# Odd heads' values in the rows of even heads' sums, one output product per tile, and gates that read a column with stride zero

## Chip, core and metric

The kernel runs on one core of one Trainium2 chip. The metric is the device time of one execution in microseconds (us); less is better. The profile records one execution: TensorE (PE, its weight loads PEld), VectorE (DVE), ScalarE (ACT), GpSimd (POOL) and SyncE (SP, which issues DMAs). All data are 32-bit floats, apart from a mask in bf16.

## What is computed

The input x has 16 batches of 256 tokens with 128 features. Six blocks are applied to it, each on a layer norm of x and each added to x:

```python
x = x + 0.5 * ffn0(layernorm(x))        # 128 -> 512 -> 512 -> 512 -> 128: silu * linear, gelu, gelu
x = x + attn0(layernorm(x))             # theta(x) phi(x)^T g(x) / sqrt(128), no softmax
x = x + 0.5 * ffn0(layernorm(x))
x = x + 0.5 * moe(layernorm(x))         # gates from the first token: top 2 of 8 experts, rank 64
x = x + attn1(layernorm(x))             # 16 heads of 8, rotary, causal softmax, W_O
x = x + 0.5 * moe(layernorm(x))
```

In attn1 each of the 16 heads has scores = q k^T / sqrt(8) under a causal mask, a softmax over the keys, and out = attn v; the heads are concatenated to 128 features and multiplied by W_O. In moe the gates are logits = first_token @ Wr^T, the two largest of 8, and a softmax over these two; the two chosen experts are merged into one 128 x 128 matrix per batch.

## The kernel before, in words

The 16 batches are worked in nine groups: seven of two batches (four tiles of 128 tokens) and two of one. Each group passes the feed-forward twice ("which" 0 and 1 in the code). The order of feed-forwards on PE is fixed: groups 0 and 1 for the first time, then alternately a second pass of group g and the first pass of group g + 2. The linear attention of a group (`nonlocal_attn`, L547) follows its first pass. After its second pass come `experts` (L644), `attention` (L703) and `after_attention` (L931).

No instruction order is written out by hand. Every piece of work is a generator that yields steps (L230) with an engine, an estimated time, buffers to take, and needs. The loop at the end of the kernel takes, again and again, the step that can begin first by its own clocks, and records its instructions; a step made with `either` (L238) takes the engine that would finish it first. Five constants steer this: LOAN (a penalty for banks 0 to 3 of PSUM), SPARED (a penalty on DVE in `either`), PATIENCE (how long exp's function table waits), SLACK (how close two steps are to count as equal), and LATE (how many of the last groups use a finer order: even heads first, and each half of the output normalised by itself). So a changed step or constant moves instructions on all engines. All recorded instructions have one line, L222, in the profile. While feed-forwards remain, PE's queue holds their products between those of the attention; when none is left, the loop adds products of `ident` by `ident` that only keep PE's clock up (`awake`, L1026).

The attention of one batch: `rotary` (L684) makes queries and keys; `maxima` (L760) makes the scores once and takes each row's maximum for each head; the negative maxima are transposed and added as a feature to the queries (`queries_with`, L805); `weighted` (L825) makes the scores again, transposed, in four rounds j of four heads each, takes exp on ACT (`softmax`, L836, reading PSUM into the tile pr) and clears the upper triangle on POOL. `values` (L868) then multiplies pr by the tile vm. For each tile of keys, vm holds 16 blocks of 32 columns, four row groups r by four rounds j. In the block of round j the eight columns at 16 * (j // 2) hold the head's values, the eight columns behind them hold ones, and the other sixteen zeros. Rounds 0 and 2 add up into one half of a PSUM bank, rounds 1 and 3 into the other half (w columns each, w = 256 queries for a whole batch). So in every 32 rows of a half there are 8 rows of outputs, 8 rows of the sums of exp that belong to them, and again 8 and 8. `output` (L849) transposes the 32 x 32 blocks (den), takes the reciprocal of two sums per block (rec), spreads it over 16 columns, transposes back (inv) and multiplies (oT). The rows with sums become 1 and meet rows of zeros in wo, which is W_O^T spread over 2 x 128 rows by `_by_half` (L1154). So the output needs two products per tile of 128 tokens, one for each half (L912 to L917).

`gated` (L582) makes the gates of a group: a product of cls (the first token's features, repeated in 128 columns) by wrT with 8 columns for each batch, then the two largest on DVE, a gather of the two experts' rows by POOL, and their product, added to ident (we). In `experts` cls is copied out of xnT, repeated, by POOL or DVE. In `gated_ahead` (L659) the first token's row y after attention is computed early and turned into a column by a product with a row of 128 ones, which gives the column repeated; ACT or DVE copies it from PSUM.

Of the kernel before, what the change touches and what calls it, by code (L numbers as in the profile page):

```python
# [20 lines left out]
P = 128  # L21
# [6 lines left out]
LANDING = 2.2  # L28
LOAN = 0.5
SPARED = 0.2  # L30
PATIENCE = 4.0
SLACK = 0.02
HOP = {"PE": 0.24, "ACT": 0.15, "DVE": 0.12, "POOL": 0.08}
# [8 lines left out]
NG = len(BATCHES)  # L42
LATE = 3
SPLIT = 0
# [12 lines left out]
def macaron_kernel(ctx: ExitStack, tc: tile.TileContext, a: dict, out: bass.AP):  # L57
# [54 lines left out]
    wvT = load("wvT", [P, D], a["wvT"], nc.sync)  # L112
    wo = load("wo", [P, 2, D], a["wo"].rearrange("(h p) d -> p h d", p=P), nc.sync)
    cosT = load("cosT", [P, S], a["cosT"], nc.sync)
# [7 lines left out]
    causal = cst.tile([P, P], F32, name="causal")  # L122
    ones = cst.tile([1, P], F32, name="ones")
    pht = cst.tile([P, D], F32, name="pht")
# [47 lines left out]
    def slots(n, name, shape):  # L172
# [14 lines left out]
        "mx": slots(2, "mx", [P, 2, P]),  # L187
    }
    extra = [cst.tile([P, 3, 2, 2 * P], F32, name=f"hS{l}") for l in (1, 2)]
    for n in ("vm", "mx", "rot"):  # L190
# [3 lines left out]
    def constants():  # L194

        yield step("POOL", 1.4, needs=(("in", 0, 0),))
        nc.gpsimd.memset(causal, 0.0)
        nc.gpsimd.affine_select(
            out=causal, in_=causal, compare_op=ALU.is_ge, fill=NEG, base=0, pattern=[[-1, P]], channel_multiplier=1
        )  # L200
        nc.gpsimd.memset(ones, 1.0)
        yield step(None, 0.0, sets=(("constants",),))

        for b in store_of["vm"]:
            yield step("POOL", 1.8)
            nc.gpsimd.memset(b.t, 0.0)
            yield step("POOL", 0.6, drop=(b,))
            for j in range(4):
                o = 8 + 16 * (j // 2)
                nc.gpsimd.memset(b.t.rearrange("p t r j c -> p (t r) j c")[:, :, j, o : o + DK], 1.0)  # L210
        for b in store_of["mx"]:
            yield step("POOL", 0.3, drop=(b,))
            nc.gpsimd.memset(b.t, 0.0)
# [368 lines left out]
    def gated(nb, cls):  # L582
# [3 lines left out]
        for b in range(nb):  # L586
            nc.tensor.matmul(pl[:, b, :], cls[:, b, :], wrT, start=True, stop=True)
        yield step("DVE", 0.5 + 0.4 * nb, drop=(bk,))
# [55 lines left out]
    def experts(sg):  # L644
        xn = yield from normed(sg.t0, sg.n, (("ffn", 0, (1, sg.t0)), ("ffn", 1, (1, sg.t0)), ("constants",)))
        xnT = yield from by_feature(sg.n, xn)
        if sg.first:
            nb = len(sg.parts)
            yield either(("POOL", 0.2 + 0.1 * nb), ("DVE", 0.1 + 0.1 * nb))
            cls = sml.tile([P, 2, P], F32, name="cls", bufs=2)  # L650
            by().tensor_copy(
                cls[:, :nb],
                xnT.t[:, : sg.n * P].rearrange("p (b s) -> p b s", b=nb)[:, :, 0:1].to_broadcast([P, nb, P]),
            )
            merged["before", sg.g] = yield from gated(nb, cls)
            yield step(None, 0.0, sets=(("before", sg.g),))
        yield from applied(("before", sg.g), sg, xnT)

    def gated_ahead(g, nb, y):  # L659
# [9 lines left out]
        for b in range(nb):  # L669
            nc.scalar.activation(  # L670
                y[:, b, :], y[:, b, :], AF.Identity, bias=shift[:1, b : b + 1], scale=rstd[:1, b : b + 1]
            )
        (bk,) = yield pe(0.22 * nb, banks=1)
        pc = bk.t[:, : 2 * D].rearrange("p (b d) -> p b d", b=2)
        for b in range(nb):
            nc.tensor.matmul(pc[:, b, :], y[:, b, :], ones, start=True, stop=True)
        yield copied(nb * D, drop=(bk,))
        cls = sml.tile([P, 2, P], F32, name="cls", bufs=2)
        copy(cls[:, :nb], pc[:, :nb])
        merged["after", g] = yield from gated(nb, cls)  # L680
# [22 lines left out]
    def attention(sg):  # L703
# [49 lines left out]
        yield either(("ACT", 0.53 + 0.225 * n), ("DVE", 0.2 + 0.135 * n), drop=(bk,), sets=(("v", sg.t0),))  # L753
        for i in range(2):
            copy(
                vm.t[:, v0 : v0 + n].rearrange("p t r (i h) c -> p (t r) i h c", i=2)[:, :, i, :, 16 * i : 16 * i + DK],
                pv[:, :n].rearrange("p t (r i h c) -> p (t r) i h c", i=2, h=2, c=DK)[:, :, i],
            )

# [65 lines left out]
        def weighted(i):  # L825
# [22 lines left out]

            def output(po, oT, m, bk, key):  # L849

                yield dve(m * 32)
                den = sml.tile([P, 16, 32], F32, name="den", bufs=1)
                nc.vector.transpose(den[:, :m].rearrange("p n c -> p (n c)"), po)
                yield step("DVE", 0.2 + 0.01 * m)
                rec = sml.tile([P, 16, 2], F32, name="rec", bufs=1)
                nc.vector.reciprocal(rec[:, :m], den[:, :m, 8::16])
                yield dve(m * 32)
                inv = sml.tile([P, 2 * S], F32, name="inv", bufs=1)
                nc.vector.transpose(
                    inv[:, : m * 32].rearrange("p (n c) -> p n c", c=32),  # L860
                    rec[:, :m].unsqueeze(3).to_broadcast([P, m, 2, 16]),
                )
                yield dve(m * 32, drop=(bk,), sets=(key,))
                nc.vector.tensor_tensor(oT, po, inv[:, : m * 32], ALU.mult)

            oT = sml.tile([P, 2 * S], F32, name="oT", bufs=3)

            def values():  # L868

                po = [None, None]  # L870
                for j in (0, 2, 1, 3):
# [15 lines left out]
                    if late and j >= 2:  # L887
                        spawn(output(pp, oT[:, half], w // 32, po[j % 2], ("oT", sg.t0, i, j)))
                    elif j == 3:
                        spawn(output(po[0].t[:, : 2 * w], oT[:, : 2 * w], w // 16, po[0], ("oT", sg.t0, i, j)))  # L890

            prs = {}
            first = True
            for j in (0, 2, 1, 3):
# [11 lines left out]
                if first:  # L906
                    spawn(values())
                    first = False
            m = q1 - q0
            (py,) = yield pe(  # L910
                0.475 * m, banks=1, needs=(("oT", sg.t0, i, 3),) + ((("oT", sg.t0, i, 2),) if late else ())
            )  # L912
# [240 lines left out]

def _by_half(w):  # L1154

    out = np.zeros((2, 4, 2, 2, DK, D), np.float32)
    out[:, :, :, 0] = w.reshape(4, 2, 2, DK, D).transpose(2, 0, 1, 3, 4)
    return out.reshape(2 * P, D)


def _layout(i):
# [20 lines left out]
        "wvT": i["L1_attn_W_V"].T,  # L1182
        "wo": _by_half(i["L1_attn_W_O"].T),
        "wv": i["L1_attn_W_V"],
# [22 lines left out]
```

## Time and profile before

| what | us |
|---|---|
| median of 3 runs | 943.13 |
| lowest and highest | 941.14, 943.76 |
| the profiled execution | 941.92 |
| its span, first to last instruction | 940.20 |
| last feed-forward product starts (us from the span's start) | 853.8 |
| last instruction of the output chain on DVE starts | 936.72 |

In the profile a line such as "pb<-wo,oT 128x128" names the tile written, the tiles read and the shape; pb is PSUM, h the feed-forward's hidden layer, T its differences, hS, h1T, h2T, w1T, w2T and w3s its weights, qkv the queries and keys, pr the exps. Each float product of the program leaves two matmul records and two weight loads. "<-" behind a row names what the engine had waited for. The granted clock of TensorE was 0.998 over the span.

### The profile page before, as it was taken

What the parts mean: (1) busy time and instruction counts of PE and PEld (TensorE: products, weight loads), DVE (VectorE), ACT (ScalarE), POOL (GpSimd) and SP (SyncE); (2) the same over time, 40 slices, a digit from 0 to 9 for tenths busy, and PEclk for the clock granted to TensorE, in tenths of its full rate; (3) what the DMA queues carried; (4) which work ended last, traced back from release to release, by engine and by line L of the source; (5) the groups of instructions that cost most, each with busy time, mean ns of one, the idle gap of its engine ahead of it and who ended that gap; (6) DMA issues with size and microseconds to landing.
All of it is one profiled execution on the core that took longest, in us unless ns stands there. A gap on an engine that the chain in (4) does not pass through costs nothing.

```text
span 940.2 us, 16493 instructions
## 1 busy us (share of the span) xinstructions
PE 906.5 (96%) x6544; PEld 682.6 (73%) x6544; DVE 653.5 (70%) x1507; ACT 458.3 (49%) x684; POOL 326.7 (35%) x508
## 2 busy tenths in 40 slices
PE   6999999999999999999999999999999999999888
PEld 4778778676776767676676867767877877777566
DVE  4744647868488485866768674894868767888783
ACT  2233533563663546544565436636455356554242
POOL 5310313311453314522343314543254243425242
PEclk9999999999999999999999999999999999999999
DMA  7100000000000000000000000000000000000000
GB/s 235 38 1 1 1 1 12 12 1 1 13 23 1 2 1 12 23 1 1 12 1 23 1 1 13 22 2 1 6 8 23 1 13 1 13 18 13 1 19 12
DMA packets 14716, 13.74 MB, mean 15 GB/s; under 512 B 2032, under 2 KB 12080, under 8 KB 14640
## 3 DMA queue, kind: packets, MB, share of 16 engines
q1 hardware_dynamic: 12624, 8.11, 2.9%
q0 software_dynamic: 1600, 4.20, 1.5%
q8 instruction: 51, 0.84, 0.4%
q10 hardware_dynamic: 416, 0.39, 0.1%
q14 instruction: 25, 0.20, 0.1%
HBM read 10.60 MB, written 2.10 MB: 14 GB/s over the span
## 4 chain that ended last, share of the span: by engine, by line
PE 68%; DVE 13%; ACT 7%; issue 4%; POOL 4%; DMA 1%; SPq 1%; POOLq 0%; DVEq 0%; ACTq 0%
PE pb L222 68%; DVE mx L222 4%; DVE pb L222 2%; ACT L222 2%; ACT pr L222 2%; ACT xn L222 2%; POOL rstd L222 1%; DVE h L222 1%; DMA w3s<-in_w3T_dram 1%; ACT h L222 1%; DVE st L222 1%; POOL pr L222 1%; POOL ve L222 1%; DVE den L222 1%; DVE inv L222 1%
## 5 line engine op out<-in xcount | busy, mean ns | idle before, releaser
L222 DVE TENSOR_TENSOR h<-h,pb 128x512 f32<-128x512 f32 (+1 forms) x180 | 112.1, 623 | 110.1 <-PE pb L222 108.4
L222 PE MATMUL pb<-T,hS 128*128 128x256 f32 (+1 forms) x576 | 132.6, 365 | 1.6 <-DVE h L222 1.2
L222 POOL TENSOR_SCALAR_AFFINE_SELECT pr<-pr 128x512 f32<-128x512 f32 x128 | 79.7, 647 | 137.3 <-ACT pr L222 137.0
L222 ACT ACTIVATE h<-h 128x512 f32<-128x512 f32 (+1 forms) x108 | 62.6, 582 | 127.3 <-DVE h L222 126.9
L222 ACT ACTIVATE pr<-pb 128x1536 f32<-128x1536 f32 x64 | 92.8, 1450 | 61.7 <-PE pb L222 50.4
L222 PE MATMUL pb<-qkv 32*128 32x256 f32 (+2 forms) x1536 | 115.2, 405 | 7.1 <-ACT pr L222 5.3
L222 DVE TENSOR_REDUCE mx<-pb 128x8 f32<-128x2048 f32 (+1 forms) x64 | 112.0, 1754 | 9.0 <-PE pb L222 8.4
L222 PEld LDWEIGHTS pb<-T,hS 128*128 128x128 f32 x576 | 97.2, 190 | 21.6 <-issue 6.7
L222 POOL TENSOR_SCALAR nm<-mv 128x4 f32<-128x4 f32 (+3 forms) x57 | 17.9, 314 | 258.1 <-DVE mv L222 256.7
L222 ACT ACT_TABLE_LOAD x72 | 92.4, 1283 | 19.6 <-PE pb L222 17.6
L222 PEld LDWEIGHTS pb<-qkv 32*128 32x128 f32 x1536 | 68.0, 184 | 39.2 <-ACT pr L222 14.0
L222 ACT ACTIVATE xn<-x,shift,rstd 128x128 f32<-128x128 f32 x130 | 54.1, 486 | 60.3 <-POOL shift L222 60.1
L222 DVE TENSOR_TENSOR pb<-pb,causal 128x1024 f32<-128x1024 f32 x54 | 66.3, 1228 | 23.5 <-PE pb L222 21.9
L222 POOL TENSOR_TENSOR T<-h 128x512 f32<-128x512 f32 (+1 forms) x45 | 50.5, 1127 | 87.1 <-ACT h L222 62.7
L222 ACT ACTIVATE sil<-pb,s 128x512 f32<-128x512 f32 (+1 forms) x72 | 44.9, 636 | 52.6 <-PE pb L222 49.7
L222 PE MATMUL pb<-xnT,w1T 128*128 128x512 f32 (+1 forms) x144 | 69.0, 561 | 1.5 <-ACT xnT L222 0.9
L222 PE MATMUL pb<-h,hS 128*128 128x256 f32 (+1 forms) x288 | 67.1, 362 | 1.4 <-DVE h L222 1.4
L222 PE MATMUL pb<-xnT,w2T 128*128 128x512 f32 (+1 forms) x144 | 68.5, 557 | 0.0
L222 POOL TENSOR_TENSOR rstd<-ve,mhalf 128x4 f32<-128x4 f32 (+3 forms) x63 | 59.4, 942 | 25.1 <-DVE ve L222 20.3
L222 PE MATMUL pb<-h,h1T 128*128 128x256 f32 (+1 forms) x288 | 68.0, 362 | 0.0
L222 PE MATMUL pb<-h,h2T 128*128 128x256 f32 (+1 forms) x288 | 66.3, 363 | 0.3 <-ACT h L222 0.3
L222 PE MATMUL pb<-T,h1T 128*128 128x256 f32 (+1 forms) x288 | 65.0, 360 | 0.1
(137 smaller groups left out, 1563.5 us busy)
## 6 DMA issues: line engine op xcount, KB each, us to landing
out_dram<-x SPq DMA_DIRECT2D x7, 256.0 KB, 2.3
x<-in_x_dram SPq DMA_DIRECT2D x6, 256.0 KB, 4.2
h1T<-in_h1T_dram SPq DMA_DIRECT2D x1, 1024.0 KB, 9.4
h2T<-in_h2T_dram SPq DMA_DIRECT2D x1, 1024.0 KB, 11.1
ab<-in_eab_dram,at POOLq DMA_INDIRECT x32, 2.8
x<-in_x_dram SPq DMA_DIRECT2D x3, 128.0 KB, 5.3
w1T<-in_w1T_dram SPq DMA_DIRECT2D x1, 256.0 KB, 3.7
w2T<-in_w2T_dram ACTq DMA_DIRECT2D x1, 256.0 KB, 3.9
```

What stands on the lines that cost most here:

```text
L222: return lambda *args, **kw: tc.keep_in_program_order(getattr(self.engine, name)(*args, **kw))
```

## The change

Odd rounds j now put their values at the columns (and so the rows) where even rounds have their ones, and the reverse. The reciprocals are written into a tile rec that stays zero elsewhere, so the spread factor is zero on rows of sums, and after the multiplication each half holds outputs in its own rows and zeros in the other's. Where both halves are normalised together, a step on POOL or DVE adds them into the first half, and the output is one product per tile with the plain W_O^T. Where they are normalised apart (the late groups), two products with the same W_O^T add up in PSUM. The values leave PSUM in one copy with a written-out access pattern where there were two. The gates ahead of attention read the first token's column of xnT as a stationary operand with stride zero; the gates behind it get one column from a product with a single one, copied by DVE, and read it with stride zero too. LOAN, SPARED, PATIENCE, SLACK and LATE get other values.

```diff
-LOAN = 0.5
-SPARED = 0.2
-PATIENCE = 4.0
-SLACK = 0.02
+LOAN = 3.0
+SPARED = 0.1
+PATIENCE = 3
+SLACK = 0.1
-LATE = 3
+LATE = 2
-    wo = load("wo", [P, 2, D], a["wo"].rearrange("(h p) d -> p h d", p=P), nc.sync)
+    wo = load("wo", [P, D], a["wo"], nc.sync)
-    ones = cst.tile([1, P], F32, name="ones")
+    ones = cst.tile([1, 1], F32, name="ones")
+    rec = cst.tile([P, 16, 4], F32, name="rec")
...
-                o = 8 + 16 * (j // 2)
+                o = 8 * (1 - j % 2) + 16 * (j // 2)
...
+        yield step("POOL", 0.2)
+        nc.gpsimd.memset(rec, 0.0)
...
-            nc.tensor.matmul(pl[:, b, :], cls[:, b, :], wrT, start=True, stop=True)
+            nc.tensor.matmul(pl[:, b, :], cls[:, b, :].to_broadcast([P, P]), wrT, start=True, stop=True)
...
-            yield either(("POOL", 0.2 + 0.1 * nb), ("DVE", 0.1 + 0.1 * nb))
-            cls = sml.tile([P, 2, P], F32, name="cls", bufs=2)
-            by().tensor_copy(
-                cls[:, :nb],
-                xnT.t[:, : sg.n * P].rearrange("p (b s) -> p b s", b=nb)[:, :, 0:1].to_broadcast([P, nb, P]),
-            )
+            cls = xnT.t[:, : sg.n * P].rearrange("p (b s) -> p b s", b=nb)[:, :, 0:1]
...
-        (bk,) = yield pe(0.22 * nb, banks=1)
-        pc = bk.t[:, : 2 * D].rearrange("p (b d) -> p b d", b=2)
+        (bk,) = yield pe(0.11 * nb, banks=1)
+        pc = bk.t[:, :nb].rearrange("p (b d) -> p b d", b=nb)
...
-        yield copied(nb * D, drop=(bk,))
-        cls = sml.tile([P, 2, P], F32, name="cls", bufs=2)
-        copy(cls[:, :nb], pc[:, :nb])
+        yield step("DVE", 0.1, drop=(bk,))
+        cls = sml.tile([P, 2, 1], F32, name="cls", bufs=2)
+        nc.vector.tensor_copy(cls[:, :nb], pc)
...
-        for i in range(2):
-            copy(
-                vm.t[:, v0 : v0 + n].rearrange("p t r (i h) c -> p (t r) i h c", i=2)[:, :, i, :, 16 * i : 16 * i + DK],
-                pv[:, :n].rearrange("p t (r i h c) -> p (t r) i h c", i=2, h=2, c=DK)[:, :, i],
-            )
+        rows = vm.t[:, v0 : v0 + n]
+        copy(
+            bass.AP(tensor=rows.tensor, offset=rows.offset, ap=[rows.ap[0], [P, n * 4], [32 + DK, 4], [1, DK]]),
+            pv[:, :n].rearrange("p t (r j c) -> p (t r) j c", j=4, c=DK),
+        )
...
-            def output(po, oT, m, bk, key):
+            def output(po, oT, m, h, bk, key):
+                both = m * 32 > w
...
+                n = w // 32
+                shape = [m // n, n, 2]
+                def places(t, at, half, block, other):
+                    return bass.AP(tensor=t.tensor, offset=t.offset + at, ap=[t.ap[0]] + [list(p) for p in zip((half, block, other), shape)])
-                nc.vector.reciprocal(rec[:, :m], den[:, :m, 8::16])
+                nc.vector.reciprocal(
+                    places(rec[:, 8 * h :], h, 8 * 4 + 1, 4, 2), places(den[:, :m], 8 * (1 - h), 32 * n - 8, 32, 16)
+                )
...
-                    rec[:, :m].unsqueeze(3).to_broadcast([P, m, 2, 16]),
+                    rec[:, 8 * h : 8 * h + m].unsqueeze(3).to_broadcast([P, m, 4, 8]),
...
+                if both:
+                    yield either(("POOL", 0.19 + 0.0021 * w), ("DVE", 0.35 + 0.0005 * w), sets=(key,))
+                    by().tensor_tensor(oT[:, :w], oT[:, :w], oT[:, w:], ALU.add)
...
+            halves = 1 + late
             for t in range(m):
-                for h in range(2):
+                for h in range(halves):
                     nc.tensor.matmul(
-                        py.t[:, t * D : (t + 1) * D], oT[:, h * w + t * P : h * w + (t + 1) * P], wo[:, h, :],
-                        start=(h == 0), stop=(h == 1),
+                        py.t[:, t * D : (t + 1) * D], oT[:, h * w + t * P : h * w + (t + 1) * P], wo,
+                        start=(h == 0), stop=(h == halves - 1),
                     )
```

More of the change, by code (lines that the diff above doesn't have):

```diff
@@ L854, in output @@
                 yield step("DVE", 0.2 + 0.01 * m)
-                rec = sml.tile([P, 16, 2], F32, name="rec", bufs=1)
-                nc.vector.reciprocal(rec[:, :m], den[:, :m, 8::16])
+                n = w // 32
[5 more added lines that the diff above has]
+                )
                 yield dve(m * 32)
@@ L860, in output @@
                     inv[:, : m * 32].rearrange("p (n c) -> p n c", c=32),
-                    rec[:, :m].unsqueeze(3).to_broadcast([P, m, 2, 16]),
+                    rec[:, 8 * h : 8 * h + m].unsqueeze(3).to_broadcast([P, m, 4, 8]),
                 )
-                yield dve(m * 32, drop=(bk,), sets=(key,))
+                yield dve(m * 32, drop=(bk,), sets=() if both else (key,))
                 nc.vector.tensor_tensor(oT, po, inv[:, : m * 32], ALU.mult)
+                if both:
+                    yield either(("POOL", 0.19 + 0.0021 * w), ("DVE", 0.35 + 0.0005 * w), sets=(key,))
+                    by().tensor_tensor(oT[:, :w], oT[:, :w], oT[:, w:], ALU.add)
             oT = sml.tile([P, 2 * S], F32, name="oT", bufs=3)
@@ L887, in values @@
                     if late and j >= 2:
-                        spawn(output(pp, oT[:, half], w // 32, po[j % 2], ("oT", sg.t0, i, j)))
+                        spawn(output(pp, oT[:, half], w // 32, j % 2, po[j % 2], ("oT", sg.t0, i, j)))
                     elif j == 3:
-                        spawn(output(po[0].t[:, : 2 * w], oT[:, : 2 * w], w // 16, po[0], ("oT", sg.t0, i, j)))
+                        spawn(output(po[0].t[:, : 2 * w], oT[:, : 2 * w], w // 16, 0, po[0], ("oT", sg.t0, i, j)))
             prs = {}
@@ L909, in weighted @@
             m = q1 - q0
+            halves = 1 + late
             (py,) = yield pe(
-                0.475 * m, banks=1, needs=(("oT", sg.t0, i, 3),) + ((("oT", sg.t0, i, 2),) if late else ())
+                0.2375 * m * halves, banks=1, needs=(("oT", sg.t0, i, 3),) + ((("oT", sg.t0, i, 2),) if late else ())
             )
             for t in range(m):
-                for h in range(2):
+                for h in range(halves):
                     nc.tensor.matmul(
-                        py.t[:, t * D : (t + 1) * D], oT[:, h * w + t * P : h * w + (t + 1) * P], wo[:, h, :],
-                        start=(h == 0), stop=(h == 1),
+                        py.t[:, t * D : (t + 1) * D], oT[:, h * w + t * P : h * w + (t + 1) * P], wo,
+                        start=(h == 0), stop=(h == halves - 1),
                     )
@@ L1151, in _tables @@
     return {n: np.ascontiguousarray(v, dtype=np.float32) for n, v in made.items()}
[L1154 to L1158, printed above, removed]
 def _layout(i):
@@ L1182, in _layout @@
         "wvT": i["L1_attn_W_V"].T,
-        "wo": _by_half(i["L1_attn_W_O"].T),
+        "wo": i["L1_attn_W_O"].T,
         "wv": i["L1_attn_W_V"],
```

## The prediction, made before the result was known

> **What bounds the kernel now.** I read the page's table of busy time first, then the busy time of each engine in stretches of the span, then what TensorE waited for, then single instructions in order of time.
>
> ```profile
> PE 906.5 (96%) x6544; PEld 682.6 (73%) x6544; DVE 653.5 (70%) x1507; ACT 458.3 (49%) x684; POOL 326.7 (35%) x508
> ```
>
> PE is the matmul row, PEld its weight loads. A share over the whole span says little, so the stretches follow. Columns: stretch, its length, then the busy time (and instructions) of PE, PEld, DVE, ACT and POOL.
>
> ```profile
> 360.00:460.00 100.00, 98.87 (x673) 72.11 (x666) 72.75 (x156) 51.40 (x79) 33.50 (x51) 1.00 0.02 6
> 560.00:660.00 100.00, 99.94 (x692) 71.65 (x690) 70.14 (x155) 57.63 (x83) 40.48 (x59) 1.00 0.03 9
> 854.00:888.00 34.00, 29.09 (x346) 19.32 (x346) 26.62 (x70) 13.53 (x17) 13.59 (x21) 1.00 0.03 9
> 888.00:941.00 53.00, 44.15 (x490) 32.70 (x486) 32.22 (x86) 15.30 (x17) 16.07 (x25) 0.98 0.05 14
> ```
>
> From 60 to 760 us TensorE is occupied 97 to 100% of every 100 us, at the full granted clock (1.00). The last feed-forward product (pb<-w3s,h) starts at 853.8. Behind it only attention of the last groups is left, and PE is busy 73.2 of 87 us (84%): there, chains through DVE, ACT and POOL set the pace. What PE waited for between 60 and 820 us is small in total (us, times, longest):
>
> ```profile
> PE pb L222 <- ACT sil L222: 4.7, 6, 1.0
> PE pb L222 <- ACT pr L222: 2.1, 5, 0.6
> PE pb L222 <- DVE h L222: 1.2, 2, 0.7
> PE pb L222 <- ACT h L222: 0.3, 1, 0.3
> ```
>
> So until about 854 us a matmul taken out shortens the program by its own time, unless its place is filled by a new wait; behind 854 us it does so only in part.
>
> **What the change moves** is seen in the order of the built instructions on each engine, since the kernel's recording loop decides that order anew. Matmuls, before to after: wo by oT 64 to 36; transposes of the maxima (ident, mx) 40 to 36; keep-warm products 76 to 83; ones by y stays 16, with one column instead of 128; gates stay 32, of which 16 read xnT directly. ACT loads its function tables 85 times instead of 73. DVE gets 64 instead of 46 of xn's tiles. Of the 28 products that go, 24 stand ahead of the last feed-forward product and 4 behind. One round of an attention batch (8 score and 8 value products) moves from behind it to ahead of it.
>
> **Prices.** A product's price in a packed PE is the distance to the start of the next group:
>
> ```profile
> 226.91 1.16 PE L222 MATMUL pb<-wo,oT 128*128 128x128 f32 x8
> 227.90 1.95 PE L222 MATMUL pb<-w3s,h 128*128 128x128 f32 x16
> 229.69 0.59 PE L222 MATMUL pb<-xnT,w1T 128*128 128x512 f32 x1
> ```
>
> ```profile
> 164.72 0.71 PE L222 MATMUL pb<-ones,y 1*128 1x128 f32 x4
> 165.36 1.13 PE L222 MATMUL pb<-h,hS 128*128 128x256 f32 x4
> 166.33 0.51 PE L222 MATMUL pb<-wrT,cls 128*128 128x8 f32 x4
> 166.69 1.11 PE L222 MATMUL pb<-T,h2T 128*128 128x256 f32 x4
> ```
>
> Each product of the program leaves two records here. Four wo products take 227.90 - 226.91 = 0.99 us, 0.248 each; eight w3s products of the same shape take 1.79, 0.224 each. I take the mean, 0.236. A product of ones and y takes 0.64/2 = 0.32; the one with 8 columns (the gates) 0.36/2 = 0.18. With one column I take 0.18, the nearest row, so 0.14 less; the bounds are 0 and 0.32 less, which is 0 to 5 us for 16. A transpose of the maxima is 0.22 (233.12 to 233.34). A round of scores is 0.87 (244.22 to 245.09), of values 0.79 (246.15 to 246.94), 1.66 together.
>
> 1. Ahead of 854 us, where PE sets the pace: 24 x 0.236 = 5.7; 14 x 0.14 = 2.0; 2 transposes 0.4; the round that moves here costs 1.7. Sum: **6.4 us less**.
> 2. Behind 854 us PE loses 4 x 0.248 + 2 x 0.14 + 2 x 0.22 + 1.66 = 3.4 us of work. It also loses a copy on a chain: POOL's cls at 861.14 (0.30 us) stood between xnT and the gates' product at 861.49. Against this, group 6 no longer counts as late (LATE 3 to 2): its outputs are normalised in one piece of 512 columns (den 0.71, reciprocal 0.35, inv 0.71, product 0.69, add 0.55 by DVE's T<-h of 128x256: 3.0 us in line), where the second half now takes 0.45 + 0.25 + 0.45 + 0.42 = 1.6; 1.4 us later for the batch that ends there. Since 16% of PE's time is idle here, the bounds are 3.4 less and 1.4 more; I take half of the removed work, **1.7 us less**.
> 3. The new adds (14, of 128x256, half on POOL, half on DVE): 0.55 on DVE, 0.73 on POOL (its T<-h of that shape). DVE in all gets about 11 us more: 18 xn tiles at 0.32, 11 more T<-h (about 7), 7 adds at 0.55, less 7 T<-h,T at 0.80. At 70 to 73% of the paced stretches that lies beside PE: 0 taken. The output products stand in the new order among w1T and w2T products, so PE has other work while it waits for the add. Without that cover, 14 x 0.7 = 9.8 us (a rival below).
> 4. Copies: the nine cls copies out of xnT go, the nine from PSUM shrink to one column per batch (DVE, 0.17 by lg<-pb 128x16, where ACT took 0.37), 18 value copies become 9 of twice the size. All are off the paced path, so 0. A stationary operand of stride zero is not in the trace of before. If each of its two weight loads took twice the 0.19 us of PEld's rows, 16 x 2 x 0.19 = 6.1 us would come on top; if loads of one repeated column were quicker, as much as 16 x 0.18 = 2.9 us would go. I take 0, since the nearest row, wrT by cls, loads as many columns.
> 5. Table loads. The twelve new ones come mostly from exps placed between the four GELUs of one layer: in ACT's order such breaks rise from 6 to 13, most of the new ones in layer two. Each puts load, exp, load = 1.28 + 1.45 + 1.28 = 4.0 us between two GELUs. Layer two of a feed-forward, in ACT's timeline of before, shows the room for it:
>
> ```profile
> 436.17 0.63 ACT L222 ACTIVATE h<-h 128x512 f32<-128x512 f32 x1
> 439.32 0.60 ACT L222 ACTIVATE h<-pb 128x512 f32<-128x512 f32 x1 [2.52 <-PE pb L222]
> 443.57 0.63 ACT L222 ACTIVATE h<-h 128x512 f32<-128x512 f32 x1 [3.65 <-DVE h L222]
> 446.37 0.63 ACT L222 ACTIVATE h<-h 128x512 f32<-128x512 f32 x1 [2.16 <-DVE h L222]
> ```
>
> ACT idles 3.65 us between the second and the third, which is where the new exp goes; 4.0 us leaves 0.4 late. Seven breaks cost 0 to 2.6 us; I take **1.0 us more**, as the new order puts some score and value products ahead of w3s.
>
> Sum: -6.4 - 1.7 + 1.0 = **-7.1 us**. The profiled execution took 941.92 us (span 940.20 and 1.72 around it), so **934.8 us**. The runs before had a median of 943.13, 1.2 more than that execution; I leave that in the range.
>
> **Rivals.**
>
> *Slower: the broken GELUs.* Place: layer two of the feed-forwards, where w3s needs all four GELUs. If PE runs out of other work there, each of 7 new breaks costs up to 4.0 us. It turns to a loss beyond 8.1/7 = 1.2 us each. At 2 us: 941.9 - 8.1 + 14 = 948; in full, 962. For it: twelve more loads are 15.4 us of ACT. Against it: PE waited only 0.3 us for GELUs in 60 to 820, although 6 breaks are there already; around one of them (ACT 363.5 to 369.5) PE was busy 8.00 of 8 us.
>
> The Trainium skill's page ScalarE: Activation LUTs (Rules for kernel authors) is on this rival's side: it says to do all work of one table set before switching, and budgets about 2.7 us for a switch. By that figure a break would be 6.8 us, seven of them 3.1 us late each, 22 us in all. The trace's loads took 1.283 us each and the next ACTIVATE began within 0.02 us of a load's end, so I keep 4.0.
>
> *No change: the product moves from PE's time to PE's wait.* If the 14 adds stand between the last value product and wo with nothing to fill, 9.8 us come back: 943.6. For it: weight loads already waited for oT in 7 places (2.7 us). Against it: the place of wo in the new order. Two engines share a part of this cost: DVE's T<-h,T (two inputs from SBUF) took 0.69 at the median and 1.78 at most, and POOL's pieces of T take 1.27, so an add may also hold up DVE by its length.
>
> That fits the Trainium skill's page SBUF — State Buffer (Who interferes with whom): a DVE instruction with two SBUF inputs and a GpSimd one that reads SBUF exclude each other for a whole instruction. By it the adds are dearer than their own length; the trace agrees, 1.78 against 0.69.
>
> *More than forecast.* If the stretch behind 854 us gives all 3.4 us, the broken GELUs cost nothing and one-column products are free (16 x 0.18 = 2.9 more): -1.7 - 1.0 - 2.9 = 929.2.
>
> That the change does not do what it says is excluded by the order: 64 products are 36.
>
> **Chances.** A measurement here can tell about 0.3% (2.8 us) from no change. Forecast, 931 to 939: 0.57. More, below 931: 0.15. No change, 939.1 to 944.7: 0.15. Slower, above 944.7: 0.13. The forecast's upper end touches no change, so faster is 0.72, same 0.15, slower 0.13. The range, 927 to 944, leaves out some 0.06 below and 0.14 above.
>
> **What would show it.** Right: 72 records of wo by oT with the stretch up to the last w3s some 6 us shorter, PE still over 98% busy there, ones by y near 0.18 to 0.2 us, and no row "PE waits for ACT h" above 2 us. Wrong: PE's waits for ACT h or DVE h grow to several us in 160 to 760 (the first rival), wo's weight loads wait for oT or POOL more than 5 us in all (the second), or the time from the last w3s to the end grows beyond 87 us.

## The result, and the profile after

The changed kernel takes 938.4 us (median of 5 runs, 938.15 to 938.6) against 943.13 (5 runs, 941.14 to 943.76): a ratio of 0.9952, 95% interval 0.9938 to 0.9965. By this ratio it is 4.5 us faster, where 7.1 less was forecast. The profiled execution's span fell from 940.2 to 936.5 us. Below, "us by ratio" of an experiment is (ratio - 1) times 942.3, the mean of the medians of the kernel before in the experiments' runs; the change itself is -4.5 by it. The intervals of these figures reach 1.0 to 1.5 us to each side, 2.2 for the slowest kernel, so a difference of two of them is known to some 1.5 to 2 us.

The busy time of the engines, from the page of after (recorded instructions now have line L226):

```profile
PE 905.6 (97%) x6498; PEld 677.2 (72%) x6498; DVE 657.9 (70%) x1527; ACT 460.7 (49%) x665; POOL 328.0 (35%) x508
```

PE has 46 records less and is still full. The stretches of after, with the columns as before (stretch, length, then PE, PEld, DVE, ACT, POOL):

```profile
360.00:460.00 100.00, 99.91 (x648) 72.78 (x646) 75.51 (x172) 53.73 (x77) 37.96 (x55) 1.00 0.03 9
560.00:660.00 100.00, 99.14 (x712) 72.50 (x711) 73.35 (x155) 53.29 (x74) 34.47 (x51) 1.00 0.03 9
852.00:888.00 36.00, 31.45 (x366) 22.19 (x366) 28.41 (x72) 11.63 (x17) 13.38 (x20) 1.00 0.03 9
888.00:938.00 50.00, 40.99 (x436) 29.66 (x436) 27.46 (x73) 14.96 (x17) 14.71 (x24) 0.94 0.05 14
```

The feed-forward's products in after, then, from two places of PE's timeline, the single products of the output and of ones by y:

```profile
L226 PE MATMUL pb<-w3s,h x512: 272/275/377, 48.6 to 851.7; 128*128 128x128 f32 x171
```

```profile
447.90 0.71 PE L226 MATMUL pb<-wo,oT 128*128 128x128 f32 x4
448.44 1.02 PE L226 MATMUL pb<-xnT,w1T 128*128 128x512 f32 x2
...
164.64 0.60 PE L226 MATMUL pb<-ones,y 1*128 1x1 f32 x4
165.17 1.13 PE L226 MATMUL pb<-T,h2T 128*128 128x256 f32 x4
```

The last w3s product starts at 851.7 us instead of 853.8, so the part up to there gives 2.1 us, where items 1 and 5 made 5.4. Of these 2.1, 0.9 is there already at the first w3s product (48.6 against 49.5 us), ahead of every product that the change touches; executions of one and the same order differ there by as much (49.1 to 50.4 in the order of before). From there to the end of the span it is 84.8 instead of 86.4, 1.6 less, where 1.7 was forecast. Two output products now take 0.54 us (0.27 each), two of ones by y 0.53 (0.27 each, not 0.18).

The 84.8 and the 86.4 are not like for like, because the granted clock differed: from 910 to 920 us it was 0.83 in after and 1.00 in before. What that costs is seen in a later experiment (one product per tile in the order of before), whose last w3s product is followed by the same matmuls as in before, and whose clock was 0.85 there. The same score products, in before and then in that execution:

```profile
917.24 0.71 PE L222 MATMUL pb<-qkv 32*128 32x256 f32 x8
...
916.87 1.18 PE L222 MATMUL pb<-qkv 32*128 32x256 f32 x8
```

From 910 to 920 us that execution falls 1.56 us behind before (starts of the same matmuls), and it needs 87.9 us from the last w3s product to the end. Against 87.9, the 84.8 of after are 3.1 less.

What PE waited for between 60 and 820 us in after (us, times, longest):

```profile
PE pb L226 <- DVE mx L226: 3.1, 5, 1.3
PE pb L226 <- DVE h L226: 1.6, 2, 1.0
PE pb L226 <- ACT pr L226: 0.5, 2, 0.4
...
PE pb L226 <- ACT sil L226: 0.2, 1, 0.2
```

The row for ACT's h (GELU) is gone; waits for ACT shrank and waits for DVE (mx, h) grew. This sum is of idle time alone, and as the experiments show most of the time lies elsewhere.

From every matmul's start to the next one's start, summed by kind up to the last w3s product, one gets where PE's time went (my sum over the trace; two records a product):

| kind | before, us (records) | after, us (records) | difference |
|---|---|---|---|
| wo by oT | 11.11 (96) | 6.14 (48) | -5.0 |
| ones by y | 4.46 (28) | 3.88 (28) | -0.6 |
| gates, both kinds | 5.88 (58) | 5.83 (58) | 0.0 |
| transposes of the maxima | 3.59 (28) | 3.76 (26) | +0.2 |
| one round moved ahead (its price in the prediction) | | | +1.7 |

These make -3.7; yet the whole came out at -2.1, because products of the same kind and number elsewhere changed their distances. The largest such kind are the products of the gathered experts (ab): 9.86 us before and 6.71 after, 58 records in both. In before, PE had to wait for ACT's sil behind them three times, 0.91, 1.02 and 0.78 us. Over time the gain isn't even. At the end of the first pass of the seventh group after is 6.45 us ahead; the next ends of passes are 5.20 and 6.59 ahead, then 3.00, then 7.55 behind, and the last two 2.07 and 2.18 ahead. Different work stands between the passes in the two orders, so these are places in time and not gains of single edits; the moved round accounts for 1.66 of them.

### The profile page after: what moved, and what is told of

The parts are those of the page before. It is cut to its first block, busy times and chain, and to the rows that moved or that the text cites. A ratio compares the mean times of both kernels' runs of the same rounds, so it can differ in the third digit from the quotient of the medians.

```text
span 936.5 us, 16393 instructions
## 1 busy us (share of the span) xinstructions
PE 905.6 (97%) x6498; PEld 677.2 (72%) x6498; DVE 657.9 (70%) x1527; ACT 460.7 (49%) x665; POOL 328.0 (35%) x508
## 4 chain that ended last, share of the span: by engine, by line
PE 75%; DVE 11%; ACT 4%; issue 4%; POOL 2%; DMA 2%; SPq 1%; POOLq 0%; DVEq 0%; ACTq 0%
PE pb L226 75%; DVE mx L226 3%; DVE h L226 1%; ACT pr L226 1%; ACT L226 1%; DMA w3s<-in_w3T_dram 1%; DVE pb L226 1%; DVE rot L226 1%; ACT xn L226 1%; DVE T L226 1%; POOL rstd L226 1%; DVE st L226 1%; DMA x<-in_x_dram 1%; ACT h L226 1%; POOL T L226 1%
## 5 line engine op out<-in xcount | busy, mean ns | idle before, releaser
L226 DVE TENSOR_TENSOR h<-h,pb 128x512 f32<-128x512 f32 (+1 forms) x180 | 111.6, 620 | 98.6 <-PE pb L226 96.6
L226 POOL TENSOR_SCALAR_AFFINE_SELECT pr<-pr 128x512 f32<-128x512 f32 x128 | 79.3, 643 | 169.1 <-ACT pr L226 141.4
L226 PE MATMUL pb<-T,hS 128*128 128x256 f32 (+1 forms) x576 | 129.2, 364 | 3.0 <-DVE h L226 2.3
L226 ACT ACTIVATE pr<-pb 128x1536 f32<-128x1536 f32 x64 | 92.8, 1451 | 64.0 <-PE pb L226 57.4
L226 PE MATMUL pb<-qkv 32*128 32x256 f32 (+2 forms) x1536 | 114.9, 406 | 5.9 <-DVE mx L226 3.0
L226 DVE TENSOR_REDUCE mx<-pb 128x8 f32<-128x2048 f32 (+1 forms) x64 | 111.9, 1749 | 4.9 <-PE pb L226 4.5
L226 PEld LDWEIGHTS pb<-T,hS 128*128 128x128 f32 x576 | 97.7, 190 | 21.6 <-issue 6.5
L226 ACT ACTIVATE h<-h 128x512 f32<-128x512 f32 (+1 forms) x108 | 61.8, 579 | 96.5 <-DVE h L226 95.9
L226 PEld LDWEIGHTS pb<-qkv 32*128 32x128 f32 x1536 | 67.9, 184 | 37.8 <-issue 10.0
L226 POOL TENSOR_SCALAR nm<-mv 128x4 f32<-128x4 f32 (+3 forms) x57 | 17.8, 312 | 205.9 <-DVE mv L226 204.6
L226 DVE TENSOR_TENSOR pb<-pb,causal 128x1024 f32<-128x1024 f32 x54 | 66.2, 1225 | 22.5 <-PE pb L226 22.4
L226 ACT ACTIVATE xn<-x,shift,rstd 128x128 f32<-128x128 f32 x112 | 46.4, 482 | 59.9 <-POOL shift L226 59.7
L226 ACT ACTIVATE sil<-pb,s 128x512 f32<-128x512 f32 (+1 forms) x72 | 45.3, 638 | 52.0 <-PE pb L226 50.1
L226 PE MATMUL pb<-xnT,w1T 128*128 128x512 f32 (+1 forms) x144 | 68.9, 560 | 1.8 <-ACT xnT L226 0.9
L226 POOL TENSOR_TENSOR T<-h 128x512 f32<-128x512 f32 (+1 forms) x34 | 39.5, 1161 | 87.1 <-ACT h L226 56.4
L226 PE MATMUL pb<-xnT,w2T 128*128 128x512 f32 (+1 forms) x144 | 69.0, 561 | 0.3
L226 POOL TENSOR_TENSOR rstd<-ve,mhalf 128x4 f32<-128x4 f32 (+3 forms) x63 | 60.0, 952 | 26.5 <-DVE ve L226 21.6
L226 PE MATMUL pb<-h,h1T 128*128 128x256 f32 (+1 forms) x288 | 67.3, 362 | 0.0
L226 PE MATMUL pb<-h,h2T 128*128 128x256 f32 (+1 forms) x288 | 67.2, 364 | 0.0
L226 PE MATMUL pb<-h,hS 128*128 128x256 f32 (+1 forms) x288 | 67.0, 361 | 0.0
L226 PE MATMUL pb<-T,h1T 128*128 128x256 f32 (+1 forms) x288 | 65.9, 359 | 0.9 <-DVE T L226 0.8
```

The costliest lines, as they stand in the source:

```text
L226: return lambda *args, **kw: tc.keep_in_program_order(getattr(self.engine, name)(*args, **kw))
```

## The experiments

Two theories at first. **Paced**: where PE's row is full, a product taken out gives its own length, and a part of the gain is lost elsewhere (order, table loads). **Local**: PE's row is full in some stretches although another engine sets the pace there; a product taken out of such a stretch gives nothing, and one of DVE's operations may cost what it takes. The recorded expectations name their own pairs (A and B, P and L, O and E) and say each time what they mean; P and L are these two. Since every edit reorders the kernel, most experiments freeze one order: they edit the instructions that a step records and keep the steps, their estimates and the constants.

**All edits in the order of before.** Steps, estimates and constants of before; the add on DVE, behind the multiplication, in its step.

```diff
-LOAN = 3.0
+LOAN = 0.5
...
-                yield dve(m * 32, drop=(bk,), sets=() if both else (key,))
+                yield dve(m * 32, drop=(bk,), sets=(key,))
                 nc.vector.tensor_tensor(oT, po, inv[:, : m * 32], ALU.mult)
                 if both:
-                    yield either(("POOL", 0.19 + 0.0021 * w), ("DVE", 0.35 + 0.0005 * w), sets=(key,))
-                    by().tensor_tensor(oT[:, :w], oT[:, :w], oT[:, w:], ALU.add)
+                    nc.vector.tensor_tensor(oT[:, :w], oT[:, :w], oT[:, w:], ALU.add)
```

> All edits of the work (odd heads' values moved, one product per tile, gates from a stride-zero column, one value copy) in the order of before: its steps, their estimated costs and the five constants stay, so that every engine's order stays but for the instructions that go or are added (the add stands on DVE right behind the multiplication; 24 products go, as LATE stays 3). Theory A, the new order gives time back: the edits alone are worth what was priced, 24 x 0.236 = 5.7 us of products, about 1 us of ones by y, and less waiting, so about 936 us (-7). Theory B, the removed products turn into waits: about 938.5 us (-4.5), as the change itself.

Measured: 943.91 us, ratio 1.0016 (1.0005 to 1.0026), +1.5 by ratio. Neither number held: the same edits that make after faster make before's order slower.

**The output's part alone, in the order of before.** Gates, ones by y and the two value copies are those of before.

```diff
+                if both:
+                    nc.vector.tensor_tensor(oT[:, :w], oT[:, :w], oT[:, w:], ALU.add)
...
-                for h in range(2):
+                for h in range(1 + late):
```

> The output part alone (24 products fewer, 12 adds on DVE) in the order of before; gates and value copies as before. Theory A: 24 x 0.236 = 5.7 us less, 937.5 us. Theory B: about 3 us less, 940 us, the rest lost to waits for the add.

Measured: 946.20 us, 1.0039 (1.0025 to 1.0053), +3.7. Neither number held. So 24 products fewer and 12 adds more are a loss of 3.7 us here, and the gates' and copies' part is worth 1.5 - 3.7 = -2.2. What PE waited for from 60 to 820 us in this kernel:

```profile
PE pb L224 <- ACT sil L224: 4.3, 6, 0.9
PE pb L224 <- DVE oT L224: 2.8, 6, 0.5
PE pb L224 <- DVE h L224: 2.5, 6, 0.7
```

Waits for oT are new (2.8 us), those for DVE's h rose from 1.2 to 2.5. What the two are worth is seen below, against kernels that have only one half of this edit.

**Two products and no adds, in the order of after.** All steps stay; the adds record nothing, and every tile gets two products.

```diff
-                    by().tensor_tensor(oT[:, :w], oT[:, :w], oT[:, w:], ALU.add)
+                    pass
...
-                for h in range(halves):
+                for h in range(2):
```

> The changed kernel in its own order and with its steps, but with no adds and with two products per tile again (28 products more, 14 adds fewer). Theory A: every product costs its time in the packed stretch, 938.4 + 24 x 0.236 + 4 x 0.1 = 944.5 us. Theory B: the products fall into waits that are there anyway, at most 941.5 us.

Measured: 940.08 us, 0.9970 (0.9957 to 0.9982), -2.8. Theory B: more than half of the gain is there without the edit that the change is about.

**The work of before with the five new constants**, planned anew.

```diff
-LOAN = 0.5
-SPARED = 0.2
-PATIENCE = 4.0
-SLACK = 0.02
+LOAN = 3.0
+SPARED = 0.1
+PATIENCE = 3
+SLACK = 0.1
...
-LATE = 3
+LATE = 2
```

> The kernel before with the five new constants alone (LOAN 3, SPARED 0.1, PATIENCE 3, SLACK 0.1, LATE 2), so that its order changes and its work does not (table loads 89 instead of 73). Theory A: the new constants cost some 3.5 us, 946.5 us. Theory B: they are worth nothing by themselves, 943 us within 1. A third possibility, that they were a gain by themselves: below 941 us.

Measured: 962.11 us, 1.0207 (1.0184 to 1.023), +19.5. No number held. By themselves the constants cost 19.5 us.

**Each single output product issued twice, in the order of after**; the second overwrites the first.

```diff
-                for h in range(halves):
+                for h in (0,) * 2 if halves == 1 else (0, 1):
```

> The changed kernel in its own order, adds and all, with each of its 28 single output products issued twice (the second overwrites the first with the same numbers). Theory P, PE paces: 28 x 0.236 = 6.6 us more, 945 us. Theory L, in these orders a product's time is partly hidden in waits for other engines: at most 941.5 us.

Measured: 941.43 us, 0.9986 (0.9976 to 0.9996), -1.3. Against after, 28 more products cost 4.5 - 1.3 = 3.2 us, 0.11 each and not 0.236. Local (L). Against the kernel with two products and no adds, the adds cost 2.8 - 1.3 = 1.5; the two intervals overlap, so this size is soft. In the traces of these two, PE's starts drift apart by only 0.5 us from 50 to 780 us, and from 795 to 800 the kernel with doubled products was granted a clock of 0.71, the other 1.00, which sets its execution back by 1.5 us more.

**One product per tile in the order of before, with no add**: the second half's product is left out, so odd heads are missing from the output of 12 of the 16 batches.

```diff
-                for h in range(2):
+                for h in range(1 + late):
```

> The kernel before in its own order without the 24 second products of the full-width batches and with no adds: the odd heads' part of the output is left out for 12 of 16 batches. Theory P: 24 x 0.236 = 5.7 us less, 937 us. Theory L: about 2 us less, 941 us, the rest going into waits.

Measured: 941.81 us, 0.9993 (0.9983 to 1.0003), -0.7, not to be told from nothing, where item 1 makes 5.7. This is the clearest blow to the paced theory, for nothing is added in return. The trace shows how the gain is lost. First the kernel before, PE's rows and DVE's row in order of time, up to the place where PE next needs a PSUM bank that DVE's product h empties:

```profile
446.99 1.16 PE L222 MATMUL pb<-wo,oT 128*128 128x128 f32 x8
447.99 1.95 PE L222 MATMUL pb<-w3s,h 128*128 128x128 f32 x16
...
453.57 1.38 DVE L222 SCALAR_TENSOR_TENSOR h<-pb,s,sil 128x512 f32<-128x512 f32 x2
...
454.34 1.13 PE L222 MATMUL pb<-xnT,w2T 128*128 128x512 f32 x2
```

Then the same place with the two wo products left out (PE's rows, from wo on, and DVE's row):

```profile
447.45 0.71 PE L222 MATMUL pb<-wo,oT 128*128 128x128 f32 x4
448.00 1.95 PE L222 MATMUL pb<-w3s,h 128*128 128x128 f32 x16
...
454.03 1.38 DVE L222 SCALAR_TENSOR_TENSOR h<-pb,s,sil 128x512 f32<-128x512 f32 x2
454.80 1.12 PE L222 MATMUL pb<-xnT,w2T 128*128 128x512 f32 x2 [0.34 <-DVE h L222]
```

There wo starts at 447.45 against 446.99 in before, and w3s behind it at 448.00 against 447.99: 0.45 us gained. But DVE's h comes at 454.03 against 453.57, and the w2T products at 454.80 against 454.34, with a wait of 0.34 that before did not have: the 0.44 is lost again, 6.3 us later. DVE worked without a break up to there and had no room to start earlier. The same gain and loss stand at this place in four groups. The second pair of wo products of these groups gains 0.45 too and loses it within 0.7 us, at transposes whose weight loads wait 0.24 to 0.25 us each for xn from ACT. In the later groups a part stays: counted from the first to the last w3s product, this execution is 1.2 us shorter than before's (50.4 to 853.5 against 49.5 to 853.8). Windows of the kernel before show that DVE is full there, not PE alone:

```profile
445.00:455.00 10.00, 9.95 (x62) 6.36 (x61) 9.97 (x21) 3.80 (x5) 1.11 (x3) 1.00 0.00 0
465.00:475.00 10.00, 10.00 (x117) 7.08 (x110) 2.81 (x6) 6.18 (x6) 4.62 (x7) 1.00 0.10 28
```

PE is busy 9.95 and 10.00 of 10 us, DVE 9.97 in the first and 2.81 in the second. Of the 120 stretches of 5 us from 160 to 760, DVE is 95% busy or more in 30 in before and in 42 in after.

**Adds that nobody reads, in before**: 12 of DVE's adds behind the multiplication.

```diff
                 nc.vector.tensor_tensor(oT, po, inv[:, : m * 32], ALU.mult)
+                if m * 32 > w:
+                    nc.vector.tensor_tensor(inv[:, :w], oT[:, :w], oT[:, w:], ALU.add)
```

> The kernel before in its own order with the 12 adds of 128x256 on DVE behind the multiplications, into a buffer that nobody reads (work added, output unchanged): nothing waits for them but DVE's own queue. Theory P, DVE has room (70% busy): 943 us within 1. Theory L, a DVE that is late by 0.55 us makes PE late: 12 x 0.3 to 0.55 us more, 946 to 949 us.

Measured: 944.84 us, 1.0029 (1.0018 to 1.0039), +2.7, 0.22 an add. Between the two numbers: on average half of an add's 0.425 us reaches the end, though nothing waits for its result. Product by product against before, it appears at the same w2T products, which start 0.44 later in each of four groups: the add ahead of this place pays in full, and the group's second add, some 37 us later, shows nowhere.

Products (-0.7) and adds (+2.7) make +2.0 of the output part's +3.7. The remaining 1.7 is about as large as what three such figures leave open. In the traces, from the first to the last w3s product, the three kernels are -1.2, +2.6 and +2.3 against before, so 0.9 remains; and from 840 to 888 us the execution of the output part was granted a clock of 0.96, the other two 1.00. The waits for oT add little of their own. In each of four groups of the output part's kernel, wo starts 0.46 later than in before, after 0.51 of waiting for oT; the missing products give 0.45 of it back; and the w2T products behind start 0.44 later, as with the idle adds. The wait uses up what the missing products give, and what reaches the end is DVE's lateness.

**The work of after with the old constants**, planned anew.

```diff
-LOAN = 3.0
-SPARED = 0.1
-PATIENCE = 3
-SLACK = 0.1
+LOAN = 0.5
+SPARED = 0.2
+PATIENCE = 4.0
+SLACK = 0.02
...
-LATE = 2
+LATE = 3
```

> The changed kernel with the five constants of before: the recording loop places the new steps with their own costs (12 adds on POOL, 40 output products, 92 table loads). If it is enough that the order is made anew for the new steps: 936 to 939 us. If the constants are a fit to one set of steps each, as the old work with the new constants (962 us) suggests: above 943 us.

Measured: 947.02 us, 1.0053 (1.0037 to 1.0069), +5.0. With the run of the old work under new constants: each set of constants fits its own work, and the other set costs 9 to 20 us.

**The work of before in the order of after**: two products, no adds, 128 ones, two value copies, the copied cls.

```diff
-            nc.tensor.matmul(pl[:, b, :], cls[:, b, :].to_broadcast([P, P]), wrT, start=True, stop=True)
+            nc.tensor.matmul(pl[:, b, :], cls[:, b, :], wrT, start=True, stop=True)
...
-                    by().tensor_tensor(oT[:, :w], oT[:, :w], oT[:, w:], ALU.add)
+                    pass
...
-                for h in range(halves):
+                for h in range(2):
```

> The work of before in the order of the change: two products per tile, no adds, two value copies, a column of ones of 128, the first token copied out of xnT (on POOL) and out of PSUM at full width (on DVE), each put where the changed kernel's step stands. Theory O, the order pays and the edits are worth next to nothing: 938 to 940 us. Theory E, the edits are worth the 4 to 5 us, but only in an order made for them: 942 to 944 us (two products without adds were 940.1 already; gates and copies were worth 943.9 - 946.2 = -2.3 us in the old order).

Measured: 942.35 us, 0.9998 (0.9987 to 1.0009), -0.2. The order alone is worth nothing that can be told (E). So the edits are worth -4.3 in it: gates and copies -(2.8 - 0.2) = -2.6, adds +1.5, products -3.2. In its trace the last w3s starts at 856.0 and the tail is 84.9 us, under a clock of 0.83 from 910 to 920 us, as in after.

**Before without the additions of the causal mask** ahead of the maxima: 54 DVE operations, 66 us of DVE, leave; the maxima then take in all keys of the block. No matmul changes.

```diff
-                    nc.vector.tensor_tensor(
-                        d, d, causal.unsqueeze(1).unsqueeze(1).to_broadcast([P, 4, 2, P]), ALU.add
-                    )
+                    pass
```

> The kernel before in its own order without the 54 DVE instructions that add the causal mask to the scores ahead of the maxima (the maxima are then taken over all keys; the mask of the softmax itself stays). 66 us of DVE's 653 go, no matmul does. If PE paces the stretch in which it is 99% busy: 941 to 943 us. If DVE paces a part of each group in spite of its 70%: 8 us less or more, below 935 us.

Measured: 937.82 us, 0.9956 (0.9944 to 0.9968), -4.1, between the two numbers. The windows of this kernel at the place shown above:

```profile
445.00:455.00 10.00, 10.00 (x57) 6.18 (x58) 7.09 (x17) 4.84 (x9) 2.92 (x5) 1.00 0.00 0
```

DVE is no longer full (7.09; only 5 of the 120 stretches stay at 95%), and 4.1 us go with no product taken out. So DVE paces a part of each group. That 66 us of it gave only 4.1 fits with PE's row, 10.00 of 10 here, being next to bind, but no run parts this from other causes.

**All 14 adds on POOL, in the order of after.**

```diff
-                    by().tensor_tensor(oT[:, :w], oT[:, :w], oT[:, w:], ALU.add)
+                    nc.gpsimd.tensor_tensor(oT[:, :w], oT[:, :w], oT[:, w:], ALU.add)
```

> The changed kernel in its own order with its 7 adds on DVE moved to POOL at the same places (all 14 on POOL). If DVE's time paces where they stand: 7 x 0.2 us less, 937 us. If the wait of the output products for the add counts instead: POOL takes 0.73 us where DVE takes 0.55, so 7 x 0.2 more, 940 us.

Measured: 939.24 us, 0.9967 (0.9954 to 0.998), -3.1: no gain over after. Relieving DVE of seven adds doesn't pay. In the trace, PE's starts against after stay where they are from 60 to 660 us (0.55 and 0.56 us later), though four of the seven adds left DVE there. One add costs: it stands on POOL behind other work, and PE waits for it.

```profile
795.82 0.71 PE L226 MATMUL pb<-wo,oT 128*128 128x128 f32 x4 [1.38 <-POOL oT L226]
```

**After with LATE 3**, planned anew.

```diff
-LATE = 2
+LATE = 3
```

> The changed kernel with LATE 3, so that group 6 is worked in the finer order as before and has two products per tile (40 in all, 12 adds); the order is made anew. If LATE 2 is what gives time back in the last groups: 935 to 937 us. If not: 938 us or, by the chance of a new order, anything up to 945.

Measured: 939.70 us, 0.9970 (0.9959 to 0.9981), -2.8. The tail is shorter by 1.6 (83.2 us), the last w3s 3.2 later (854.9). LATE 2 isn't what gives the time back. No variant of after was faster than after.

## Why the prediction was partly right

Sign and range held; the size was 4.5 for 7.1. Of its signs of being right, the 72 records of wo, PE's share (98 to 100% of every 100 us from 60 to 760) and PE's waits for GELUs came; the 6 us up to the last w3s (2.1 came) and ones by y near 0.18 to 0.2 us (0.27) did not. By its own steps:

1. **The premise of item 1 failed**: "until about 854 us a matmul taken out shortens the program by its own time". The read distances were right (0.248 a product; 5.0 us of them are gone in the trace). But 24 products alone gave 0.7 us in the old order, which can't be told from nothing, and 28 gave 3.2 in the new one, 0.11 each. A full PE row with small waits does not show that PE sets the pace: at 454.34 us of before the weight loads of w2T had waited 0.72 us for DVE's h, and PE's row shows no idle time there. The new order has the wo products among w1T and w2T, not just ahead of a stretch that DVE fills. Against the kernel with doubled products, the first pair of a group keeps its 0.45 us there, and the second loses 0.28 of it at the transposes behind it.

   The Trainium skill says in Perfetto Trace Analysis (Identifying the Most-Contended Engine) that the share of busy time of matmuls is no good measure of how close a kernel is to the peak, since they are pipelined, and that the busy share of weight loads tells more. The trace agrees as to the first: PE is at 97 to 100% in the stretches taken for paced, PEld at 71 to 83%, and products were worth at most half of their length. But PEld hardly parts the two windows above, 6.36 and 7.08 of 10 us.

2. **Ones by y were mis-sized** in item 1: -0.6 us, not -2.0. One column takes 0.28 a product on average (3.88 us for 14), not 0.18: the row with a stationary operand of one partition was nearer than the gates' row with eight columns. The transposes gave +0.2 for -0.4. The moved round was right.

3. **The tail's number came out right by luck.** 84.8 us is 1.6 less than before's 86.4, but under a lower clock; against the 87.9 of an execution with the same matmuls there and nearly the same clock it is 3.1 less, close to item 2's bound of 3.4 and not to half of it. Nor is it the removed work that gave it: the old work in the new order has 84.9, and two products per tile or doubled ones in the new order 84.8 each, with 4 products more behind the last w3s. So it comes with the order. The moved round (1.66) is about half of the 3.1; the 1.4 for LATE 2 is near the 1.6 by which the run with LATE 3 has a shorter tail, though that has another order. The rest stays open.

4. **Item 3, adds at 0, failed in the old order and may hold in the new one.** POOL's price was right (0.727 for 0.73) and DVE's too high (0.425 for 0.55), as the trace of after shows. In the old order the adds cost 2.7 us unread and 4.4 where wo needs them (3.7 + 0.7; 3.5 by the traces up to the last w3s). In the new one they cost 1.5 by ratio, soft as said, and 0.5 in the traces up to 780 us. "At 70 to 73% of the paced stretches that lies beside PE" is the same error as in 1: 70% is a mean over stretches at 100 and at 28%.

```profile
L226 POOL TENSOR_TENSOR oT<-oT x7: 721/727/732, 230.0 to 862.9; 128x256 f32<-128x256 f32 x7
L226 DVE TENSOR_TENSOR oT<-oT x7: 424/425/426, 261.5 to 882.9; 128x256 f32<-128x256 f32 x7
```

   That an add may hold up the other engine, as the prediction feared, is shown too. In after, four of POOL's T<-h,T start within 0.1 us of a DVE add and take 1.48 us each, where they take 1.26 to 1.27 in the kernels with no adds and with all adds on POOL; and one of DVE's T<-h,T of 128x256, beside an add on POOL, takes 0.93 us instead of the 0.43 of the kernel with no adds.

5. **Item 4, gates and copies at 0, failed in the other direction.** They gave 2.2 in the old and 2.6 us in the new order, of which ones by y explain 0.6. Stride zero itself was right at 0: PE's weight loads from the column read with stride zero (after) are as long as those from the copied, repeated column (before).

```profile
L226 PEld LDWEIGHTS pb<-wrT,xnT x32: 185/190/192, 137.7 to 864.2; 128*128 128x128 f32 x32
L222 PEld LDWEIGHTS pb<-wrT,cls x64: 186/192/192, 139.6 to 901.1; 128*128 128x128 f32 x64
```

   In the new order the traces place a part of the rest. In the old work PE waits twice for POOL's copy of cls, 0.68 us at 674.61 and 0.38 at 759.06; where the gates read xnT directly, those waits are 0.22 and nothing, and PE gains 0.46 at each place. In the old order, where the rest lies stays open.

6. **Item 5, broken GELUs at +1.0, was too dear**, and the first rival with it. PE's wait for GELUs between 60 and 820 us went from 0.3 us to none, with twelve more loads. One of the breaks, on ACT in after:

```profile
434.54 1.28 ACT L226 ACT_TABLE_LOAD   x1
435.83 1.45 ACT L226 ACTIVATE pr<-pb 128x1536 f32<-128x1536 f32 x1
437.30 1.28 ACT L226 ACT_TABLE_LOAD   x1
438.59 1.15 ACT L226 ACTIVATE h<-h 128x512 f32<-128x512 f32 x2
```

   4.0 us, as priced, and PE has other products over it. The Trainium skill's rule in ScalarE: Activation LUTs (Rules for kernel authors) is to finish the work of one table set first. No run takes these loads alone, but PE's waits show no cost of them here: none for GELUs, and 0.5 us for pr where before had 2.1.

Of the rivals, the second ("from PE's time to PE's wait") came nearest in the old order: there the output's part is a loss. In the new order it isn't, as the prediction argued from the place of wo. What it lacked was that most of the lost time is a wait for DVE's other work, not for the add's result. The terms of the sum against the runs in the new order: products -3.2 for -5.7 (2.5 missing), adds +1.5 for 0 (1.5 missing), gates, ones and copies together -2.6 for -2.0 (0.6 more), and all that the order does (round, tail, transposes, GELUs) -0.2 for +0.6 (0.8 more): -7.1 + 2.5 + 1.5 - 0.6 - 0.8 = -4.5. The runs' terms are differences of neighbouring runs, so they add up by construction, and each is known to some 1.5 to 2 us. That the whole came within 3 us of the forecast is in part luck, since errors of 4.0 one way met 1.4 the other way. Open: why the new order gives back 4 to 6 us in its last groups, how much of the 4.5 us depends on where the granted clock fell, and which constant matters.

## What to carry to other kernels

Before a removed matmul is credited with its length, look at windows as short as a loop's phases: two engines full in the same window mean that the busy row alone can't tell which one paces. Freeze the order and take the operation out or issue it twice; this gives its price directly, and here it was at most half of the distance in the trace, and in one order not to be told from nothing. Before two tails are compared, look at the granted clock in each. Where a planner decides the order, an edit and its constants are one change: each alone made this kernel slower.

## What the runs showed of the hardware

A matmul's time here hardly fell with its columns where the stationary operand has one partition: 0.32 us a product with 128 columns, 0.28 with one. A stationary operand of stride zero loads in 190 ns, a contiguous one in 192. DVE adds 128x256 floats from SBUF in 0.425 us, POOL in 0.727. The two engines can hold each other up: one DVE add that ran beside POOL's T<-h and T<-h,T took 0.832 us (the output part in the old order), and POOL's T<-h,T beside a DVE add 1.48 us instead of 1.27. Where the granted clock fell, to 0.85 over 10 us, eight score records took 1.18 us instead of 0.71.
